# A two-layer decoder on one core: order of layers, score banks, units in flight and seven-product layers

## The chip, the cores and the metric

The kernel runs on one core of a Trainium2 chip. The metric is device time in microseconds (us) of that core. TensorE (PE) multiplies matrices and transposes; its results go to PSUM, of which the kernel uses eight banks of 128 x 512 fp32. VectorE (DVE) and ScalarE (ACT) read PSUM; GpSimd (POOL) doesn't in this kernel. SyncE (SP) issues most of the loads.

## What is computed

Six sublayers one after the other, each followed by a residual addition and a layer norm, all in fp32, on 16 sequences of 128 tokens with 256 features:

```python
x = _layernorm(x + attn0(x))       # 16 heads of 64, causal
x = _layernorm(x + xattn0(x))      # 8 experts, relu, gate made from ctx and itok: all 8 for every token
x = _layernorm(x + ffn0(x))        # 2 shared experts; 2 of 16 routed experts for each token
x = _layernorm(x + attn1(x))       # 16 heads of 16, keys within 8 of the query
x = _layernorm(x + xattn1(x, ctx)) # 16 heads of 16, keys and values from ctx
x = _layernorm(x + ffn1(x))        # 8 experts, gelu, gated sum: all 8 for every token
```

The experts of `xattn0` and `ffn1` each map 256 features to 512 and back.

## The kernel before

The 16 sequences are four groups (g = 0 to 3) of four sequences, 512 tokens. A piece of work is written (layer, g): (0,g) the first attention, (1,g) the first mixture of eight experts, (2,h) the routed mixture for half h, that is two groups at once, (3,g) and (4,g) the two attentions with 16-wide heads, (5,g) the last mixture of eight. A group passes its layers in order; (2,1) needs the routing of groups 2 and 3, so both (1,2) and (1,3), and (3,2) needs (2,1).

**Order.** Pieces are Python generators. They yield an estimated TensorE time, or a due time (`UNTIL`), or a condition. A planner (`Weaver.weave`) draws from a main stream (attention), a side stream called `dense` (mixtures) and a list of short ones (transposes, gates, routing plans, collecting results). Short streams go first; of main and side, the one with the smaller share of work done so far, each share divided by a given number of us. A stream that is not due, or whose condition doesn't hold, is passed over, and the other goes on and its share grows. The order so written is the priority of instructions; a scheduler of the language, in front of the chip, then fixes each engine's order and takes tiles' slots from pools, so an instruction that would lack a slot comes later. The dense order is a list near the end of the function (the line with `dense = Stream(chain(`), followed by the calls that weave: (0,0), (0,1) alone; (0,2), (0,3) with dense; then (3,0), (4,0); (3,1), (4,1); (3,2), (4,2), (3,3), (4,3); and what remains of dense.

**PSUM.** `bank` (L49) gives one bank for anything but attention scores, from six; scores take a pair of banks (tag S), of which there is one. So six and two make eight.

**16-wide attention.** `attention16` works through eight units of one sequence and half of the heads. For each, `scores` masks the keys by head on POOL (`kb`, L515), multiplies on TensorE and hands the scores to `softmax`, which on DVE and ACT makes a weight tile `e` (three slots, tag p); its scaling by `inv` (L380) is on POOL. Two steps later in the loop come the transposes of the weights (`weights_T`, ACT copy L390), one step after it the product with the values (`weigh`), and one more step later the output projection.

**Mixtures of eight.** `products` computes for each expert two matrix products. The second one (`multiply`, L836) always multiplies block matrices with seven products in place of eight, with block sums on DVE (L812 to L815); their weights' block sums are made on POOL once (L696 and L699) and kept in HBM. The first product, `hidden`, takes for each expert eight matmuls of 128x512 (each is two instructions in the trace), four banks, and one pass of DVE (L942, layer 1) or ACT (L1365, layer 5) per bank. With a `Firsts` object, the experts after the first use seven block products here too: 14 matmuls of 128x256, a bank `sums` that lives through the whole expert, two more banks, three ACT copies (L777, L782, L786), three DVE additions (L771), and the weights' sums (`weight_sums`, recorded at L720 and L746) as four POOL operations an expert; `rows_sums` adds four DVE operations per layer. Before, (5,2) and (5,3) have this, and no (1,g).

**Routed mixture.** `plan` ends with 16 scatters by indirect DMA on POOL (L1127); `experts0` runs two shared experts for two groups, then 16 pairs of routed tiles whose rows are loaded from what was scattered; `collect` gathers (L1303, POOL), adds and normalizes.

Of the kernel before, what the change touches and what calls it, by code (L numbers as in the profile page):

```python
# [8 lines left out]
F32 = mybir.dt.float32  # L9
# [5 lines left out]
P = 128  # L15
D = 256
# [6 lines left out]
T = GB * P  # L23
# [8 lines left out]
def kernel(ctx: ExitStack, tc: tile.TileContext, a: dict, out: bass.AP):  # L32
# [11 lines left out]
    ps = ctx.enter_context(tc.tile_pool(name="psum", bufs=2, space=bass.MemoryType.PSUM))  # L44
# [2 lines left out]


    def bank(tag):  # L49
        return ps.tile([P, T], F32, tag="B", name=f"ps{tag}", bufs=6)  # L50

    recent = [None]

# [8 lines left out]
    def joined(first):  # L62

        return nullcontext() if first else tc.high_priority()
# [38 lines left out]
    def load_quad(j):  # L103

        cols = slice(j * D, (j + 1) * D)
        return load_w(
            "attn", 2048, f"wquad{j}", a["L0_attn_W_Q"][:, :, cols], a["L0_attn_W_K"][:, :, cols],
            a["L0_attn_W_V"][:, :, cols], a["L0_attn_W_O"][:, 2 * j:2 * j + 2, :],
        )
# [206 lines left out]
    def project(pt, w, cols, xT):  # L316

        for c in range(KC):
            mm(pt, lhsT=w[:, c, cols], rhs=xT[:, c, :], start=c == 0, stop=c == KC - 1)
# [76 lines left out]
    def attention0(x, g):  # L396
        norm = Norm(x)
        norm.bias(bo0)

        def project_quad(g, j):  # L400
            wq, wk, wv, wo = first_quads[j] if g == 0 and j < 2 else load_quad(j)
            xT = xTs[g]
            qT = p2.tile([P, 2, T], F32, tag="qT", name="qT")
            kT = p2.tile([P, 2, T], F32, tag="kT", name="kT")
            for i in range(2):
                c = 2 * j + i
                cols = slice(i * P, (i + 1) * P)
                pq = bank("H")
                project(pq, wq, cols, xT)
                nc.vector.tensor_scalar(  # L410
                    qT[:, i, :], pq, bq0[:, c:c + 1], 0.125, ALU.add, ALU.mult
                )
                pk = bank("H")
                project(pk, wk, cols, xT)
                nc.scalar.activation(kT[:, i, :], pk, AF.Identity, bias=bk0[:, c:c + 1])
                yield 3.44

            v = yield from values(xT, wv, KC)
            heads0[g, j] = qT, kT, v, wo

        def scores(j, b):
            qT, kT, _, _ = heads0[g, j]
            at = slice(b * P, (b + 1) * P)
            s = ps.tile([P, 2, T], F32, tag="S", name="psS", bufs=1)[:, :, :D].rearrange(
                "p s (i k) -> p s i k", i=2
            )

            for i in range(2):
                for k in range(2):
                    rows = slice(64 * k, 64 * k + 64)  # L430
                    with joined(i == k == 0):
                        mm(
                            s[:, k, i, :], lhsT=qT[rows, i, at], rhs=kT[rows, i, at],
                            start=True, stop=True,
                        )
            return softmax(s, causal)

        def output(j, b, zT):
            po = bank("H")[:, :D]
            for i in range(2):  # L440
                mm(po, lhsT=zT[:, i, :], rhs=heads0[g, j][3][:, i, :], start=i == 0, stop=i == 1)
            norm.add(b, po, last=j == 3)

        if (g, 0) not in heads0:
            yield from project_quad(g, 0)
        units = [(j, b) for j in range(4) for b in range(GB)]
        e, eT, zT, at = {}, {}, {}, {}
        for n in range(len(units) + 5):
            if n < 16:
                j, b = units[n]  # L450
                e[n] = scores(j, b)
                at["e", n] = weaver.now + 9.0
                yield 0.6
            m = n - 2
            if m in e:
                yield UNTIL, at["e", m]
                eT[m], _ = weights_T(e.pop(m))
                at["t", m] = weaver.now + 2.5
                yield 0.5
            m = n - 5  # L460
            if m in zT:
                yield UNTIL, at["z", m]
                output(*units[m], zT.pop(m))
                yield 0.86
            m = n - 4
            if m in eT:
                j, b = units[m]
                yield UNTIL, at["t", m]

                pz = bank("O")[:, :D].rearrange("p (c q) -> p c q", c=2)  # L470
                got = eT.pop(m)
                for i in range(2):
                    for k in range(2):
                        h = 2 * i + k
                        with joined(h == 0):
                            mm(
                                pz[64 * k:64 * k + 64, i, :],
                                lhsT=heads0[g, j][2][:, b, 64 * h:64 * h + 64],
                                rhs=got[:, 2 * k + i, :], start=True, stop=True,
                            )  # L480
                zT[m] = p3.tile([P, 2, P], F32, tag="z", name="zT")

                nc.vector.tensor_tensor(  # L483
                    zT[m], pz, bv0[:, 2 * j:2 * j + 2].unsqueeze(2).to_broadcast([P, 2, P]), ALU.add
                )
                at["z", m] = weaver.now + 2.5
                yield 0.6
            if n < 16 and (n < 12 or g + 1 < NG):

                j, b = units[n]  # L490
                if b == 0:
                    ahead = project_quad(g, j + 1) if j < 3 else project_quad(g + 1, 0)
                yield next(ahead)
                if b == 3:
                    assert next(ahead, None) is None
        assert not e and not eT and not zT
        norm.done()


    def attention16(x, qT, kT, v, bv, wo, bo, seen):  # L500
# [9 lines left out]
        def scores(b, c):  # L510

            at = slice(b * P, (b + 1) * P)

            kb = p2.tile([P, 4, P], F32, tag="kb", name="kb")
            nc.gpsimd.tensor_tensor(  # L515
                kb, kT[:, c, at].unsqueeze(1).to_broadcast([P, 4, P]),
                hm4.unsqueeze(2).to_broadcast([P, 4, P]), ALU.mult,
            )
            yield UNTIL, weaver.now + 2.0
            s = ps.tile([P, 2, T], F32, tag="S", name="psS", bufs=1)  # L520
            s = s[:, :, :4 * keys].rearrange("p s (h k) -> p s h k", h=4)
            for k in range(2):
                rows = slice(64 * k, 64 * k + 64)
                for queries, key, _ in parts:
                    mine = slice(b * P + queries.start, b * P + queries.stop)
                    with joined(k == 0 and key == 0):
                        mm(
                            s[queries, k], lhsT=qT[rows, c, mine],
                            rhs=kb[rows, :, key:key + keys], start=True, stop=True,
                        )  # L530
            return softmax(s, seen)
# [37 lines left out]

        units = [(b, c) for b in range(GB) for c in range(2)]  # L570
        e, eT, zT, at = {}, {}, {}, {}
        for n in range(len(units) + 5):
            if n < 8:
                e[n] = yield from scores(*units[n])
                at["e", n] = weaver.now + 12.0
                yield 1.06
            m = n - 2
            if m in e:
                yield UNTIL, at["e", m]
                got = e.pop(m)  # L580
                eT[m] = [weights_T(got[:, 4 * k:4 * k + 4, :]) for k in range(2)]
                at["t", m] = weaver.now + 3.5
                yield 1.0
            m = n - 4
            if ("z", m) in at and units[m][1] == 1:
                yield UNTIL, at["z", m]
                output(units[m][0])
                yield 0.86
            m = n - 3
            if m in eT:  # L590
                yield UNTIL, at["t", m]
                weigh(*units[m], eT.pop(m))
                at["z", m] = weaver.now + 3.0
                yield 0.63
# [337 lines left out]
    def ensemble0(x, xT, g):  # L932
# [13 lines left out]
        def done(to, got, e, i, j):  # L946
# [10 lines left out]
            lambda t: after(  # L957
                products_end(t, norm, None, lambda norm, b: norm.done(b, 2)), tail(1, g)
            ),
            Firsts(xT, done) if g in () else None,  # L960
        )

    def small(tag, n=16, bufs=None):
# [391 lines left out]
    def experts1(x, xT, g, ng):  # L1355
# [16 lines left out]
        for b in range(GB):  # L1372
# [4 lines left out]
        yield from products(  # L1377
            load, lambda e: load_blocks(1, e, g, a["L1_ffn_w2"][e]), hidden,
            lambda t: after(products_end(t, norm, ng, lambda norm, b: store(norm, g, b))),
            Firsts(xT, done) if g in (2,3) else None,  # L1380
        )


# [69 lines left out]
    def begin(g):  # L1453
# [6 lines left out]

    weaver.short += [Stream(begin(g)) for g in range(NG)]
    dense = Stream(chain(
        (1, 0), (1, 1), (2, 0), (1, 2), (1, 3), (2, 1), (5, 0), (5, 1), (5, 2), (5, 3),
    ))
    weaver.short += [Stream(fill_tables()), Stream(sum_last_blocks())]
    weaver.weave(Stream(chain((0, 0), (0, 1))))
# [75 lines left out]
```

## Time and profile before

| | us |
|---|---|
| median of 3 runs | 1738.57 |
| lowest, highest | 1735.91, 1738.95 |
| the profiled execution | 1738.27 |
| its span, first to last instruction | 1736.6 |

The profile is of one execution. Where pieces lie in it, from the times of their own instructions:

| from | to | what runs |
|---|---|---|
| 0 | 217 | (0,0), (0,1) |
| 217 | 544 | (1,0), (1,1), with (0,2) and much of (0,3) |
| 544 | 610 | routing and scatters of half 0, rest of (0,3) |
| 610 | 676 | (2,0) |
| 676 | 1016 | (1,2), (1,3), with (3,0), (4,0), (3,1) |
| 1016 | 1146 | routing and scatters of half 1, (2,1), with (4,1) |
| 1146 | 1541 | (5,0), (5,1), start of (5,2), with (3,2), (4,2), (3,3), (4,3) |
| 1541 | 1736.6 | rest of (5,2), (5,3) |

Two more rows of the page, each digit the tenths of one fortieth of the span (43.4 us): how busy DVE is, and the clock that TensorE was granted.

```profile
DVE  4565565576677534878796875858769675965655
...
PEclk9999999999998899999999989999999999999998
```

In a groups row stand: line, engine, operation, output<-inputs, size of the weights, shape, count; after the bar the busy us of the group, the mean ns of one, the idle us of the engine just before them and what ended it. A matmul's ns include the end of its pipeline, so the next one starts before it is over. A stage row has start and end, length, then busy us (instructions) of PE, PE weight loads, DVE, ACT, POOL, then the granted clock, the DMA engines' share and GB/s. A chain row has start, length, and what the chain stood on.

### The profile page before, as it was taken

Reading aid. Unit: us, or ns where it says so; the run is one execution under the profiler, and the core shown is the slowest. Engines: PE = TensorE matmul, PEld = TensorE weight load, DVE = VectorE, ACT = ScalarE, POOL = GpSimd, SP = SyncE. Lnnn points to the kernel's source line nnn. Section 1 sums busy time; section 2 is a strip of 40 time slices with the busy share of each in tenths; the row PEclk is TensorE's granted clock in tenths of the full one; section 3 lists DMA queues with packets and bytes.
Section 4 is the critical chain, followed back from the end, with each engine's and each line's share of the span. In section 5 each row is a group of like instructions: output and inputs, shape, how many; then the busy total and the mean of one; then the engine's idle time right before and its main releaser. Section 6 shows DMA issues by size and latency. Waiting matters only on the chain.

```text
span 1736.6 us, 22830 instructions
## 1 busy us (share of the span) xinstructions
PE 1647.3 (95%) x8196; PEld 1080.5 (62%) x8196; DVE 1164.0 (67%) x2330; ACT 591.8 (34%) x1360; POOL 505.5 (29%) x543
## 2 busy tenths in 40 slices
PE   9999999999999799999899988998999999999996
PEld 6665656666656465656556655665665665588785
DVE  4565565576677534878796875858769675965655
ACT  4434411111022242103131212643846372654342
POOL 5443532220002302312241315334224132522220
PEclk9999999999998899999999989999999999999998
DMA  9533533432330458422223204671222221124330
GB/s 272 174 118 123 172 140 111 150 112 103 103 110 13 146 186 290 153 93 82 90 79 104 80 31 170 202 245 64 68 91 80 71 70 67 63 83 134 113 121 34
DMA packets 98192, 204.52 MB, mean 118 GB/s; under 512 B 16136, under 2 KB 58176, under 8 KB 98016
## 3 DMA queue, kind: packets, MB, share of 16 engines
q1 hardware_dynamic: 92176, 179.53, 31.2%
q0 software_dynamic: 5904, 23.54, 3.7%
q8 instruction: 65, 1.06, 0.2%
q14 instruction: 47, 0.39, 0.1%
HBM read 172.43 MB, written 37.81 MB: 121 GB/s over the span
## 4 chain that ended last, share of the span: by engine, by line
PE 75%; DVE 12%; DMA 4%; issue 3%; POOL 2%; ACT 1%; SPq 1%; another core or an unknown queue 0%; POOLq 0%; DVEq 0%; ACTq 0%
PE psH L55 40%; PE psM L55 21%; PE psO L60 5%; PE psS L55 4%; PE psO L55 3%; PE psH L60 2%; DVE nmax L358 1%; DVE e L364 1%; DMA wquad<-in_L_attn_W_Q 1%; DMA rows<-copies 1%; DVE total L370 1%; DVE x L311 1%; DVE x L293 1%; DVE acc L836 1%; POOL got L1303 1%
## 5 line engine op out<-in xcount | busy, mean ns | idle before, releaser
L55 PE MATMUL psH<-xT,we 128*128 128x512 f32 (+1 forms) x856 | 397.4, 590 | 0.5 <-DMA we<-in_L_xattn_proj_in 0.5
L380 POOL TENSOR_TENSOR e<-e,inv 128x512 f32<-128x512 f32 (+2 forms) x121 | 159.4, 1319 | 425.6 <-DVE inv L378 369.7
L55 PE MATMUL psM<-cm,wb 128*128 128x256 f32 x1024 | 263.6, 381 | 0.0
L55 PEld LDWEIGHTS psH<-xT,we 128*128 128x128 f32 x856 | 156.8, 191 | 137.0 <-issue 124.9
L55 PEld LDWEIGHTS psM<-cm,wb 128*128 128x128 f32 x1024 | 192.0, 190 | 52.2 <-issue 25.7
L55 PE MATMUL psM<-h,wb 128*128 128x256 f32 x768 | 200.8, 384 | 5.0 <-ACT h L1365 3.4
L836 DVE TENSOR_TENSOR acc<-psM,acc 128x512 f32<-128x512 f32 (+1 forms) x216 | 134.5, 624 | 98.3 <-PE psM L55 98.2
L390 ACT COPY eT<-psO 128x512 f32<-128x512 f32 (+1 forms) x192 | 105.5, 584 | 275.6 <-PE psO L60 261.3
L55 PEld LDWEIGHTS psM<-h,wb 128*128 128x128 f32 x768 | 143.0, 190 | 54.8 <-issue 29.3
L373 ACT ACTIVATE e<-e,nmax 128x128 f32<-128x128 f32 x256 | 99.5, 390 | 139.6 <-DVE nmax L358 113.4
L942 DVE SCALAR_TENSOR_TENSOR h<-psH,gt 128x512 f32<-128x512 f32 x128 | 87.6, 685 | 71.5 <-PE psH L55 71.2
L55 PE MATMUL psH<-xT,wquad 128*128 128x512 f32 x256 | 117.2, 601 | 6.1 <-DMA wquad<-in_L_attn_W_Q 5.4
L515 POOL TENSOR_TENSOR kb<-kT,hm 128x512 f32<-128x512 f32 x64 | 72.4, 1134 | 159.1 <-PE psS L55 104.5
L60 PEld LDWEIGHTS psO<-ident,e 128*128 128x128 f32 (+1 forms) x768 | 85.2, 133 | 48.2 <-issue 35.9
L60 PE MATMUL psO<-ident,e 128*128 128x128 f32 (+1 forms) x768 | 109.7, 280 | 2.0 <-POOL e L380 2.0
L1365 ACT ACTIVATE h<-psH,b 128x512 f32<-128x512 f32 (+1 forms) x100 | 60.6, 623 | 104.7 <-PE psH L55 95.9
L369 ACT ACTIVATE e<-e 128x576 f32<-128x576 f32 (+1 forms) x64 | 55.7, 871 | 88.2 <-DVE e L364 87.9
L55 PEld LDWEIGHTS psH<-xT,wquad 128*128 128x128 f32 x256 | 46.7, 190 | 58.9 <-issue 47.8
L309 POOL TENSOR_TENSOR rstd<-ve,mhalf 128x4 f32<-128x4 f32 (+1 forms) x32 | 28.9, 903 | 177.9 <-DVE ve L307 177.6
L370 DVE TENSOR_REDUCE total<-e 128x8 f32<-128x576 f32 (+1 forms) x64 | 62.8, 981 | 24.6 <-ACT e L369 24.0
L55 PE MATMUL psO<-eT,v 128*64 128x128 f32 (+2 forms) x1024 | 76.6, 313 | 0.0
L55 PE MATMUL psH<-wquad,zT 128*128 128x256 f32 x256 | 67.8, 388 | 4.8 <-DVE zT L483 2.5
(240 smaller groups left out, 2624.0 us busy)
## 6 DMA issues: line engine op xcount, KB each, us to landing
wb<-wbd SPq DMA_DIRECT2D x56, 896.0 KB
we<-in_L_xattn_proj_in SPq DMA_DIRECT2D x32, 512.0 KB
wt<-table SPq DMA_DIRECT2D x64, 256.0 KB
we<-in_L_ffn_w SPq DMA_DIRECT2D x32, 512.0 KB
wbd<-wb POOLq DMA_DIRECT2D x16, 896.0 KB
gt<-gatesd SPq DMA_DIRECT2D x32, 256.0 KB
results<-y SPq DMA_DIRECT2D x10, 768.0 KB
rows<-copies SPq DMA_DIRECT2D x6, 1024.0 KB
```

The costliest lines, as they stand in the source:

```text
L55: recent[0] = nc.tensor.matmul(*args, **how)
L60: return nc.tensor.transpose(out_, in_, ident[:n, :n])
L309: nc.gpsimd.tensor_tensor(rstd[:, at], ve[:, at], mhalf[:, at], ALU.pow)
L369: nc.scalar.activation(e, e, AF.Exp)
L370: nc.vector.tensor_reduce(total, e, AX.X, ALU.add)
L373: nc.scalar.activation(e[:, h, :], s[:, h // (n // 2), h % (n // 2), :], AF.Exp, bias=nmax[:, h:h + 1], accum_out=total[:, h:h + 1],)
L380: engine.tensor_tensor(e, e, inv.unsqueeze(2).to_broadcast([P, n, keys]), ALU.mult)
L390: return eT, nc.scalar.copy(eT, pt)
L515: nc.gpsimd.tensor_tensor(kb, kT[:, c, at].unsqueeze(1).to_broadcast([P, 4, P]), hm4.unsqueeze(2).to_broadcast([P, 4, P]), ALU.mult,)
L836: nc.vector.tensor_tensor(to, pm[:, :len(slots), :], to, ALU.add)
L942: nc.vector.scalar_tensor_tensor(out=h, in0=ph, scalar=0.0, in1=gates[e], op0=ALU.max, op1=ALU.mult)
L1365: nc.scalar.activation(to, one, AF.Gelu, bias=b1[:, 4 * e + c:4 * e + c + 1])
```

## The change

Five places change. The common banks go from six to four and the score pairs from one to two (in `attention0` as well as `attention16`). In `attention16` transposes, output and weighing of a unit come three, five and four steps after its scores, where they came two, four and three, and the loop has one step more. `Firsts` is given to (1,0), (1,1) and (5,1) too. In the dense order (5,0) stands before (2,1).

```diff
     def bank(tag):
-        return ps.tile([P, T], F32, tag="B", name=f"ps{tag}", bufs=6)
+        return ps.tile([P, T], F32, tag="B", name=f"ps{tag}", bufs=4)
...
-            s = ps.tile([P, 2, T], F32, tag="S", name="psS", bufs=1)[:, :, :D].rearrange(
+            s = ps.tile([P, 2, T], F32, tag="S", name="psS", bufs=2)[:, :, :D].rearrange(
...
-            s = ps.tile([P, 2, T], F32, tag="S", name="psS", bufs=1)
+            s = ps.tile([P, 2, T], F32, tag="S", name="psS", bufs=2)
...
-        for n in range(len(units) + 5):
+        for n in range(len(units) + 6):
...
-            m = n - 2
+            m = n - 3
             if m in e:
...
-            m = n - 4
+            m = n - 5
             if ("z", m) in at and units[m][1] == 1:
...
-            m = n - 3
+            m = n - 4
             if m in eT:
...
-            Firsts(xT, done) if g in () else None,
+            Firsts(xT, done) if g in (0,1) else None,
...
-            Firsts(xT, done) if g in (2,3) else None,
+            Firsts(xT, done) if g in (1,2,3) else None,
...
     dense = Stream(chain(
-        (1, 0), (1, 1), (2, 0), (1, 2), (1, 3), (2, 1), (5, 0), (5, 1), (5, 2), (5, 3),
+        (1, 0), (1, 1), (2, 0), (1, 2), (1, 3), (5, 0), (2, 1), (5, 1), (5, 2), (5, 3),
     ))
```

## The prediction

> **What bounds the kernel now.** I read the page's busy rows first, then a table of stages, then the chain of waits. The page's first row puts TensorE at the limit of the whole run:
>
> ```profile
> PE 1647.3 (95%) x8196; PEld 1080.5 (62%) x8196; DVE 1164.0 (67%) x2330; ACT 591.8 (34%) x1360; POOL 505.5 (29%) x543
> ```
>
> The stage table (start and end, length, busy time of each engine with its instructions, granted clock, DMA share, GB/s) shows where that fails:
>
> ```profile
> 217.00:544.00 327.00, 325.29 (x1393) 205.84 (x1391) 209.26 (x403) 53.97 (x191) 62.70 (x86) 1.00 0.32 112
> 544.00:610.00 66.00, 52.30 (x287) 34.97 (x287) 39.77 (x116) 22.55 (x86) 18.49 (x19) 0.84 0.29 96
> 610.00:676.00 66.00, 60.46 (x342) 42.74 (x341) 24.20 (x66) 27.11 (x76) 0.00 (x0) 0.95 0.67 229
> 1016.00:1146.00 130.00, 110.37 (x620) 72.32 (x619) 84.94 (x202) 51.21 (x118) 44.05 (x36) 0.89 0.49 160
> 1200.00:1541.00 341.00, 331.34 (x1723) 204.91 (x1722) 257.05 (x460) 192.75 (x263) 111.88 (x92) 0.99 0.22 75
> ```
>
> To price a stage I need matmul work, not busy time. A gapless stretch near the end of the chain gives the unit:
>
> ```profile
> 1690.12 2.59 PE psM L55 x12
> ...
> 1696.16 3.45 PE psM L55 x16
> ```
>
> All of these are 128x256, so one takes 0.216 us. The timeline's start-to-start of the 128x512 ones is 0.43 us, of full 128x128 ones 0.109; the tiled small ones I count at 0.03 to 0.23, also from start-to-start. Counting each stage's forms at these prices gives work and loss: 217 to 544, 309 and 18; 544 to 610, 40 and 26; 610 to 676, 49 and 17; 676 to 1016, 313 and 27; 1016 to 1146, 88 and 42; 1146 to 1541, 357 and 38; the rest, 176 and 20. With 38 before 217, some 1512 is work and 225 is loss.
>
> The largest loss, 1016 to 1146, is in the chain of waits of that stage:
>
> ```profile
> 1034.16 10.69 PE psH L55 x20
> ...
> 1046.58 20.94 issue
> ...
> 1072.39 6.96 DMA wt<-table
> ```
>
> Mixture (1,3) has ended, (2,1) needs its plan and its sixteen scatters, and only the attention (4,1) is left. Its key masks and softmax scaling are on POOL, which sits behind those scatters (16 x 0.96 us). Here the Trainium skill (Perfetto Trace Analysis, Identifying the Most-Contended Engine) calls matmul busy time a bad measure and asks for LDWEIGHTS busy. By the busy row this stage loses 19.6 us. LDWEIGHTS is busy 56% of it, and 88% in the gapless end (80.5 of 92 us), which would make the loss 47. My count, 42, keeps the forms apart, and I use it.
>
> **Sevens in three more layers, (1,0), (1,1), (5,1).** Each of seven experts of a layer trades 16 instructions of 128x512 (6.88 us) for 28 of 128x256 (6.04 us): 0.84 x 7 x 3 = 17.6 us less work. What they add is read from (5,2) and (5,3):
>
> ```profile
> L771 DVE TENSOR_TENSOR h<-psM,h x42: 640/692/692, 1523.8 to 1711.7; 128x512 f32<-128x512 f32 x42
> ...
> L720 POOL TENSOR_TENSOR sw<-we x28: 723/728/982, 1470.9 to 1686.6; 128x256 f32<-128x256 f32 x28
> ```
>
> DVE: 3 x 0.69 per expert and 4 x 0.42 per layer, 16 us a layer. POOL: 4 x 0.73 = 2.9 per expert. ACT: 3 x 0.58 per expert. In 217 to 544 DVE goes from 209 to 241 in about 315 us, 77%; POOL and ACT have room. TensorE covers them while attention (0,2), (0,3) has work to offer; with that cover gone each late addition would cost its 0.69 us, 29 us for two layers at the very worst. In (5,1) the weight sums on POOL queue between the sixteen gathers of (2,1) (0.96 each, behind the landing of the results, 4.9 us): at most one expert late. I take 2.6 us of stalls in all, so -15; bounds -18 and 0.
>
> **(5,0) ahead of (2,1).** (5,0) depends on (4,0), normalized at 929, so it can start at 1016. Its loads (0.5 MB and 0.9 MB an expert, 11 MB in all) pass on SP ahead of (2,1)'s row and table loads; at a DMA share of 0.49 they fit, and (2,1)'s loads no longer wait for the scatters. On POOL it issues three additions at the end (0.8 us each), so the scatters don't hold it. Beside it runs (4,1): 103 + 29 = 132 us of work, loss taken as 8. Then (2,1) stands alone, for (3,2) needs its result. The trace has that case: (2,0) alone, 610 to 676, lost 17. From its end to the first projections of (3,2) took some 45 us before (gathers, norm, transposes); (5,1) covers it. After that (3,2) to (4,3) have only what is left of (5,1), some 50 us, and (5,2), 97, beside 124 of their own, where they had some 210 before. The planner's shares count what dense work ran while they were blocked, so attention now goes first and dense pieces fill its due times, about 30 us a layer; some of (5,2) should be left to cover the start of (5,3). Loss for the stage: 38 before, 45 after, for the mix is tighter. Sum: 42 + 38 against 8 + 17 + 45, so -10; bounds -34 (nothing more lost in the lone stage or the tighter mix) and +20.
>
> **Two score banks, four common ones.** Waits of score matmuls for a reader of the one bank, from the groups view (5.5 and 3.9 and 2.2 us):
>
> ```profile
> L55 PE MATMUL psS<-kT,qT 64*128 64x128 f32 x512 | 47.0, 303 | 5.5 <-DVE e L352 5.5
> L55 PE MATMUL psS<-kb,qT 64*128 64x512 f32 x128 | 37.2, 657 | 7.5 <-DVE e L364 3.9 <-issue 3.4
> L55 PE MATMUL psS<-kb,qT 64*64 64x288 f32 x256 | 22.9, 427 | 2.4 <-DVE e L352 2.2 <-DVE inv L378 0.2
> ```
>
> 11.6 us is the most this can return; part turns into the next wait, so -4. Against it stands the skill's same page (Optimization Strategy): repeated gaps on the engine that should be full can mean too little SBUF or PSUM for the next tile, and this edit takes two of six common banks. Pairing each group of matmuls with its reader in the timeline, a bank of the main forms lives 1.7 to 3.5 us; four or more are in use 1% of 217 to 544, 15% of 1155 to 1268, 7 to 10% up to 1448 and 0 to 6% of most other stages, 65 us in all. By the rule all of that is exposed, and if a third of it stalls it costs 22; by the pairing a fifth bank is seldom asked for. A layer of sevens in the gapless end had at most two of these plus its own two. I take +6, bounds 0 and +22.
>
> **Three 16-wide units in flight.** No instruction is added; transposes, weighing and output of a unit come one step later in the order. Nothing in the trace shows a fourth softmax tile, and there are still three of tag p, so the fourth unit's softmax waits on the first one's transposes; behind that wait on DVE would stand other evacuations, each under 1.2 us. TensorE's waits for softmax results in these layers are small (2.0 for `e` on L380, 3.0 for `zT`). I take -2, bounds -8 and +6.
>
> **Sum.** -15 - 10 - 4 + 6 - 2 = -25. The profiled execution took 1738.27 (span 1736.6, 1.7 around it) and the median is 1738.57, so the two agree to 0.3: 1713.
>
> **The rivals.** About 0.2%, 3.5 us, is what a measurement of this kernel can tell from no change.
> - *The holes close fully* (0.17). (2,1)'s gaps find work, the tighter mix loses nothing: order -34, the rest -15, near 1689. For: PE loses only 18 in 217 to 544, where two streams of work run. Against: (2,0) alone did lose 17.
> - *The sevens are eaten by DVE and the late order gains nothing* (0.18). DVE is at 75% in 1200 to 1541 and 83% from 850 to 1016; if the additions come late TensorE gets 6 of 17.6, order -2, score banks -4, common banks +6, units -2: near 1730. Against: the gapless end shows the sevens themselves costing no gap.
> - *No change* (0.07). Only the reordering's loss cancels it all, 1735 to 1742: the order doesn't do what it says because (3,2) starts about 70 us later.
> - *Slower, by the attention chain* (0.13). From (2,1)'s end to (4,3)'s norm it took 395 us (1146 to 1541). (2,1) would now end near 1212 (1016, less 10 for the sevens before it, plus 140 and 66); with 121 us behind the chain ((5,3) with its end 109, its transposes and gate 12, uncovered) the kernel breaks even at 404. Were the chain set by latency, not by TensorE, and each of its four layers lengthened 6 us by missing banks, it takes 419, a span of 1752 and a time of 1754. For: nothing but (5,1) and (5,2) can cover it. Against: PE is busy 331 of 341 there with 310 of work, and over 60 us of that dense work has gone elsewhere, so it should shrink toward 345.
>
> **How the numbers follow.** The case of the sum, 1700 to 1725, has 0.45. Faster is 0.45 + 0.17 + 0.18 = 0.80, same 0.07, slower 0.13. The range 1692 to 1738 takes in the first three cases and half of no change, leaving out the chain rival and the best end.
>
> **What would show it.** The 42 us hole at the end of (1,3) gone, with first-product work of (5,0) at once behind it; a lone (2,1) of about 66 us, some 1146 to 1212; 336 instructions of 128x512 fewer and 588 of 128x256 more, over three layers; psS waits for DVE under 5 us; no new waits of `psH` or `psM` matmuls for their readers over 10 us. I am wrong if TensorE idles after the last (4,3) unit, if L771 leaves ACT and TensorE waiting in (1,0) and (1,1), or if bank waits pass 20 us.

## The result and the profile after

The changed kernel takes 1751.20 us, median of 5 runs (1749.95 to 1755.85), against 1738.95 of the kernel before in the same measurement: a ratio of 1.0077, with a 95% interval of 1.0061 to 1.0094. By the ratio it is slower by 13 us, where 25 us less were forecast. The profiled execution, the slowest of the five, took 1755.85 us, its span 1754.2, so the two profiled spans differ by 17.6 us.

TensorE has less to do, and its busy row hardly changes (1647.3 before):

```profile
PE 1645.9 (94%) x8448; PEld 1129.2 (64%) x8448; DVE 1221.8 (70%) x2412; ACT 637.2 (36%) x1455; POOL 564.4 (32%) x620
```

252 matmul instructions more (588 of 128x256 in, 336 of 128x512 out) are less work: counted at the prices of the prediction, 1494 us where it was 1512. So the loss, time in which TensorE doesn't work at full clock, went from 225 to 260. Here it is by stage, work and loss in us:

| stage | before | work, loss | after | work, loss | loss forecast |
|---|---|---|---|---|---|
| to the end of (0,1) | 0 to 217 | 179, 38 | 0 to 212 | 178, 34 | 34 |
| to the end of (1,1) | 217 to 544 | 309, 18 | 212 to 528 | 296, 20 | 20 |
| plan of half 0, (2,0) | 544 to 676 | 89, 43 | 528 to 663 | 91, 44 | 43 |
| (1,2), (1,3) | 676 to 1016 | 313, 27 | 663 to 1012 | 316, 33 | 25 |
| then | 1016 to 1146, (2,1) with (4,1) | 88, 42 | 1012 to 1174, (5,0) with (4,1) | 143, 19 | 8 |
| | | | 1174 to 1243, (2,1) alone | 52, 17 | 17 |
| to (4,3)'s norm | 1146 to 1541 | 357, 38 | 1243 to 1613 | 301, 69 | 45 |
| the rest | 1541 to 1737 | 176, 20 | 1613 to 1755 | 118, 24 | 20 |

(The column on the right divides the forecast's terms over the stages; 6 us for banks were not placed.) In the stage rows of the kernel after, columns as before, the lone (2,1) behaves like the lone (2,0), and the stage of the last attention layers has lost clock as well:

```profile
1012.00:1174.00 162.00, 151.49 (x659) 94.55 (x659) 115.20 (x238) 68.68 (x92) 36.96 (x35) 0.97 0.30 100
1174.00:1243.00 69.00, 61.91 (x346) 42.63 (x345) 29.67 (x88) 28.01 (x77) 1.40 (x2) 0.98 0.69 231
1238.00:1613.00 375.00, 342.03 (x1881) 238.01 (x1882) 286.11 (x510) 209.45 (x344) 166.97 (x152) 0.96 0.23 77
1613.00:1754.00 141.00, 121.24 (x555) 101.25 (x553) 89.37 (x177) 47.03 (x96) 31.97 (x39) 0.96 0.26 89
```

The same two stages before, from (2,1)'s last pair to (4,3)'s norm and on to the end:

```profile
1140.00:1541.00 401.00, 386.87 (x1938) 237.98 (x1938) 294.68 (x555) 209.95 (x291) 138.04 (x115) 0.99 0.26 88
1541.00:1737.00 196.00, 178.34 (x821) 152.08 (x819) 117.53 (x227) 72.87 (x150) 42.22 (x55) 0.96 0.29 96
```

(2,1) ends 98 us later, the attention layers behind it take only 26 us less, and what follows them 55 less: 17 us in all. The signs by which the forecast was to be known came with this loss all the same: the hole behind (1,3) is mostly gone (loss 42 to 19), (2,1) runs alone for 69 us, and the instruction counts are as said. They show that the edits took effect, not that they pay. Score matmuls wait less for DVE, 4.7 us where it was 11.6:

```profile
L55 PE MATMUL psS<-kT,qT 64*128 64x128 f32 x512 | 46.2, 302 | 2.4 <-DVE e L352 2.0 <-issue 0.3
L55 PE MATMUL psS<-kb,qT 64*128 64x512 f32 x128 | 36.1, 641 | 3.2 <-issue 2.4 <-DVE e L364 0.7
L55 PE MATMUL psS<-kb,qT 64*64 64x288 f32 x256 | 22.7, 427 | 2.0 <-DVE e L352 2.0
```

But a kind of wait appears that the kernel before hardly had: a matmul that waits for the reader of somebody else's tile. TensorE's waits, from 663 to 1012 and, behind the dots, from 1243 to 1454 (total, times, longest):

```profile
PE psO L55 <- DVE acc L836: 1.2, 1, 1.2
PE psH L60 <- DVE h L942: 0.9, 1, 0.9
PE psO L55 <- DVE h L942: 0.8, 1, 0.8
...
PE psM L55 <- DVE h L771: 2.8, 2, 2.1
PE psH L55 <- POOL sw L720: 2.8, 1, 2.8
PE psO L55 <- ACT h L1365: 2.6, 1, 2.6
PE psH L55 <- ACT h L1365: 2.2, 1, 2.2
```

A product with values, `psO`, takes nothing from an expert's hidden tile `h`. It waits for the bank that the operation writing `h` has read and gives back. With six common banks (the first kernel below) no `psO` waits for an `h` any more. `psM <- h L771` and `psH <- sw L720` are different: there the sevens of (5,1) wait for their own additions and weight sums.

### The profile page after: what moved, and what is told of

The parts are those of the page before. It is cut to its first block, busy times and chain, and to the rows that moved or that the text cites. A ratio compares the mean times of both kernels' runs of the same rounds, so it can differ in the third digit from the quotient of the medians.

```text
span 1754.2 us, 23714 instructions
## 1 busy us (share of the span) xinstructions
PE 1645.9 (94%) x8448; PEld 1129.2 (64%) x8448; DVE 1221.8 (70%) x2412; ACT 637.2 (36%) x1455; POOL 564.4 (32%) x620
## 4 chain that ended last, share of the span: by engine, by line
PE 66%; DVE 20%; DMA 3%; ACT 3%; issue 3%; POOL 2%; another core or an unknown queue 1%; SPq 1%; POOLq 0%; DVEq 0%; ACTq 0%
PE psH L55 34%; PE psM L55 22%; PE psO L60 3%; PE psO L55 3%; DVE e L364 2%; DVE nmax L358 2%; PE psS L55 2%; DVE total L370 2%; PE psH L60 2%; DVE acc L836 1%; DVE cm L812 1%; DVE cm L814 1%; DVE cm L813 1%; DVE x L311 1%; DMA rows<-copies 1%
## 5 line engine op out<-in xcount | busy, mean ns | idle before, releaser
L55 PE MATMUL psM<-cm,wb 128*128 128x256 f32 x1024 | 266.9, 385 | 4.3 <-DVE cm L812 2.4
L55 PE MATMUL psH<-xT,we 128*128 128x512 f32 (+1 forms) x604 | 259.0, 557 | 7.0 <-ACT h L1365 2.2
L380 POOL TENSOR_TENSOR e<-e,inv 128x512 f32<-128x512 f32 (+2 forms) x114 | 150.4, 1320 | 301.8 <-DVE inv L378 266.9
L55 PEld LDWEIGHTS psM<-cm,wb 128*128 128x128 f32 x1024 | 191.9, 191 | 52.1 <-issue 14.1
L55 PE MATMUL psM<-h,wb 128*128 128x256 f32 x768 | 206.0, 392 | 4.5 <-ACT eT L390 2.0
L55 PEld LDWEIGHTS psH<-xT,we 128*128 128x128 f32 x604 | 112.7, 193 | 97.8 <-issue 77.9
L55 PEld LDWEIGHTS psM<-h,wb 128*128 128x128 f32 x768 | 145.6, 194 | 46.3 <-issue 16.4
L55 PE MATMUL psH<-xT,wquad 128*128 128x512 f32 x256 | 119.0, 609 | 3.9 <-DMA wquad<-in_L_attn_W_Q 3.5
L60 PE MATMUL psO<-ident,e 128*128 128x128 f32 (+1 forms) x768 | 112.1, 280 | 8.8 <-ACT eT L390 4.4
L60 PEld LDWEIGHTS psO<-ident,e 128*128 128x128 f32 (+1 forms) x768 | 85.2, 133 | 52.2 <-issue 24.9
L771 DVE TENSOR_TENSOR h<-psM,h 128x512 f32<-128x512 f32 x105 | 72.1, 687 | 42.4 <-PE psM L55 40.2
L720 POOL TENSOR_TENSOR sw<-we 128x256 f32<-128x256 f32 x70 | 56.5, 807 | 115.9 <-PE psM L55 92.3
L55 PE MATMUL psO<-eT,v 128*64 128x128 f32 (+2 forms) x1024 | 77.1, 315 | 9.4 <-ACT h L1365 4.7
L1303 POOL DMA_INDIRECT got<-results,r_places x32 | 31.9, 996 | 166.5 <-DMA we<-in_L_xattn_proj_in 84.6
L55 PEld LDWEIGHTS psH<-xT,wquad 128*128 128x128 f32 x256 | 47.3, 192 | 56.9 <-issue 50.6
L1365 ACT ACTIVATE h<-h,b 128x256 f32<-128x256 f32 x126 | 57.5, 501 | 70.2 <-DVE h L771 64.7
```

The costliest lines, as they stand in the source:

```text
L55: recent[0] = nc.tensor.matmul(*args, **how)
L60: return nc.tensor.transpose(out_, in_, ident[:n, :n])
L380: engine.tensor_tensor(e, e, inv.unsqueeze(2).to_broadcast([P, n, keys]), ALU.mult)
L720: engine.tensor_tensor(to, one, two, ALU.subtract)
L771: nc.vector.tensor_tensor(block(i, j), other, block(i, j), ALU.add)
L1365: nc.scalar.activation(to, one, AF.Gelu, bias=b1[:, 4 * e + c:4 * e + c + 1])
```

## The experiments

Each ratio is to the kernel before, run on the same chip in the same measurement, with its 95% interval. "Undone" edits start from the changed kernel, "alone" ones from the kernel before. All leave the computation as it is. The kernel before took 1730 us in the measurement of the first four kernels and 1739 to 1740 in the others, so ratios are compared here, not times. The traces place this difference ahead of (2,0), and not by edit but by measurement: from the start of the last scatter of half 0, those four reach the first matmul of the shared experts within 2 us, and all the others, the kernel before and the changed one among them, after 9 to 14. In the changed kernel's trace ScalarE stands still for 16.1 us there; for what, the trace doesn't name.

Theory A was: four common banks are too few. Theory B: the later (2,1) makes the last four attention layers a chain bound by latency. Theory C: sevens in (5,1) load DVE and ACT beside attention.

### One part undone

Banks as before (the score tile of `attention0` likewise):

```diff
-        return ps.tile([P, T], F32, tag="B", name=f"ps{tag}", bufs=4)
+        return ps.tile([P, T], F32, tag="B", name=f"ps{tag}", bufs=6)
...
-            s = ps.tile([P, 2, T], F32, tag="S", name="psS", bufs=2)
+            s = ps.tile([P, 2, T], F32, tag="S", name="psS", bufs=1)
```

> The changed kernel with its banks as before: six common ones and one pair for scores. Theory A (four common banks are too few once sevens hold one through a whole expert beside attention; matmuls wait for readers of unrelated tiles): the waits on readers of other tiles after 1243 go, time 1712 to 1728. Theory B (the later (2,1) makes the four last attention layers a chain bound by latency): the banks matter little, 1743 to 1755. Theory C (sevens in (5,1) load DVE and ACT beside attention): 1740 to 1752.

Measured 1.0042 (1.0019 to 1.0064). Of the 0.77% some 0.35 goes, where A wanted more than the whole. On the 1739 us of the first measurement it would be 1746, which B and C both allow.

The old order:

```diff
-        (1, 0), (1, 1), (2, 0), (1, 2), (1, 3), (5, 0), (2, 1), (5, 1), (5, 2), (5, 3),
+        (1, 0), (1, 1), (2, 0), (1, 2), (1, 3), (2, 1), (5, 0), (5, 1), (5, 2), (5, 3),
```

> The changed kernel with the old order, (2,1) ahead of (5,0). Theory A: the hole of 42 us at 1016 comes back, the bank waits stay, so 1748 to 1765. Theory B: the chain is started 70 us earlier and covered by (5,0), (5,1) and part of (5,2), so 1715 to 1730. Theory C: 1745 to 1758, as (5,1) still runs beside attention.

Measured 1.0031 (1.0019 to 1.0043). A wanted it slower; the order costs. But B alone wanted 1% or more to go.

Two units in flight again (steps n - 2, n - 4, n - 3, and one loop step less):

```diff
-            m = n - 3
+            m = n - 2
             if m in e:
...
```

> The changed kernel with two 16-wide units in flight. Theories A, B and C all put it within 6 us of 1751. If three units in flight were what costs (transposes, weighing and output come later in the order and hold their banks and tiles longer), it is 1735 or less.

Measured 1.0181 (1.0156 to 1.0205). None of the theories as written had this: the depth, which I had booked at -2 us, saves 1.0% in this company. In the traces the chain from (2,1)'s last matmul to (4,3)'s norm takes 392 us with two units and 373 with three.

Eight products in (5,1):

```diff
-            Firsts(xT, done) if g in (1,2,3) else None,
+            Firsts(xT, done) if g in (2,3) else None,
```

> The changed kernel with eight products in (5,1), sevens in (1,0), (1,1), (5,2), (5,3). Theory C: 1730 to 1740, since (3,2) and (4,2) then share DVE and ACT with lighter work. Theory A: part of it, 1743 to 1752 (a bank less is held, but 6 us of work come back). Theory B: (5,1) is longer cover, 1745 to 1752.

Measured 1.0016 (1.0000 to 1.0033): 6 us of matmul work come back and the kernel gets 0.6% faster. On 1739 us that is 1742, between what C and what A and B wanted, so the time alone doesn't decide. The stage does: the rows from (2,1)'s end to (4,2)'s norm, first with eight products in (5,1), then the changed kernel's:

```profile
1233.00:1430.00 197.00, 185.00 (x895) 111.11 (x894) 144.79 (x266) 91.28 (x126) 83.58 (x68) 0.97 0.27 94
```

```profile
1243.00:1454.00 211.00, 188.04 (x982) 130.02 (x981) 159.32 (x286) 105.28 (x174) 103.08 (x96) 0.94 0.27 88
```

The sevens put 14.5 us more on DVE, 14.0 on ACT and 19.5 on POOL, and the stage is 14 us longer. That speaks for C.

### One part alone

Banks (both score tiles):

```diff
-        return ps.tile([P, T], F32, tag="B", name=f"ps{tag}", bufs=6)
+        return ps.tile([P, T], F32, tag="B", name=f"ps{tag}", bufs=4)
...
-            s = ps.tile([P, 2, T], F32, tag="S", name="psS", bufs=1)
+            s = ps.tile([P, 2, T], F32, tag="S", name="psS", bufs=2)
```

> The kernel before with four common banks and two pairs for scores, nothing else. If four banks are too few by themselves it is 1.005 to 1.012 of before. If they cost only where sevens run beside attention (which undoing shows in the sum: 0.35% less), it is 0.998 to 1.003. If a second pair for scores frees attention, 0.990 to 0.997.

Measured 1.0072 (1.0051 to 1.0092): the swap costs by itself.

Four common banks, one score pair:

```diff
-        return ps.tile([P, T], F32, tag="B", name=f"ps{tag}", bufs=6)
+        return ps.tile([P, T], F32, tag="B", name=f"ps{tag}", bufs=4)
```

> The kernel before with four common banks and still one pair for scores: two banks of PSUM unused. If the 0.72% of the swap of banks is the missing common banks, this is 1.007 to 1.015, the second pair giving some back; if the second pair itself disturbs the order, 0.999 to 1.004.

Measured 1.0140 (1.0121 to 1.0159). So the two missing banks cost 1.4%, 24 us, and the second pair gives back 0.7%, 12 us. TensorE's waits of this kernel from 1010 to 1460 again name readers of banks, most of them of other tiles:

```profile
PE psM L55 <- DVE acc L836: 2.6, 1, 2.6
...
PE psO L60 <- DVE x L291: 1.7, 1, 1.7
PE psH L60 <- DVE zT L559: 1.4, 1, 1.4
...
PE psO L60 <- DVE acc L836: 0.6, 1, 0.6
```

They sum to a few us only. The rest is not in waits that the trace names. The scheduler that fixes each engine's order knows of the four slots and puts off what would lack one, which fits what is seen, though it was not tried apart: work simply comes later, (4,1)'s norm at 1160 where it was 1155, (3,2)'s at 1280 (1269), (4,3)'s at 1562 (1541).

Order:

```diff
-        (1, 0), (1, 1), (2, 0), (1, 2), (1, 3), (2, 1), (5, 0), (5, 1), (5, 2), (5, 3),
+        (1, 0), (1, 1), (2, 0), (1, 2), (1, 3), (5, 0), (2, 1), (5, 1), (5, 2), (5, 3),
```

> The kernel before with (5,0) ahead of (2,1), nothing else. Theory B (the four last attention layers are a chain that starts later and has less work beside it): 1.004 to 1.015 of before. The prediction's sum (the hole at 1016 filled, the later stage hardly worse): 0.992 to 0.996.

Measured 1.0108 (1.0057 to 1.0159), against the prediction's term of -10 us and for B. From (2,1)'s last pair to (4,3)'s norm, and to the end:

```profile
1243.00:1624.00 381.00, 349.07 (x1856) 227.87 (x1856) 285.71 (x501) 204.35 (x311) 147.77 (x128) 0.98 0.24 80
1624.00:1753.00 129.00, 109.17 (x496) 90.82 (x495) 77.39 (x165) 42.41 (x85) 28.25 (x35) 0.94 0.26 86
```

By the same count of forms this stage has 323 us of work, 39 less than before, and is 20 us shorter: its loss went from 39 to 58. The longest of TensorE's waits in it are for weight tiles of attention, `PE psO L60 <- POOL e L380`, 13.5 us in five waits.

Depth (and one loop step more):

```diff
-            m = n - 2
+            m = n - 3
             if m in e:
...
-            m = n - 4
+            m = n - 5
...
-            m = n - 3
+            m = n - 4
```

> The kernel before with three 16-wide units in flight, nothing else. If depth alone is what gains (undoing it in the changed kernel cost 1%): 0.988 to 0.994. If it gains only with the second pair of score banks, since one pair is handed from unit to unit, or only where the cover is thin: 0.997 to 1.004.

Measured 1.0044 (1.0031 to 1.0056): alone it costs.

Depth and banks, the two edits shown above, together.

> The kernel before with four common banks, two score pairs and three 16-wide units in flight. Alone these gave 1.0072 and 1.0044. If they are independent, 1.010 to 1.013. If depth pays once there are two score pairs (undoing the depth in the changed kernel cost 1.0%): 0.992 to 1.000.

Measured 1.0082 (1.0062 to 1.0102). A second score pair doesn't make depth pay, so that is not where the 1.0% comes from.

Depth and order, likewise.

> The kernel before with the new order and three 16-wide units in flight; banks and sevens as before. If the new order costs because the last four attention layers are a chain bound by latency, depth shortens it: 1.002 to 1.008 of before, where the order alone gave 1.0108. If the two costs are independent (1.0108 and 1.0044): 1.013 to 1.018.

Measured 1.0046 (1.0028 to 1.0065), where the two alone would sum to 1.015. Depth costs 0.4% in the old order and saves 0.6% in the new one, with banks and sevens as before. The two intervals in the new order overlap a little (1.0057 to 1.0065), but the pair with all else changed, 1.0181 and 1.0077, agrees and is clear. That speaks for B: depth lets an attention layer run further ahead of its own softmax, and only in the new order does that shorten the kernel. In the old order, too, the chain behind (2,1) takes 387 us instead of 397 with it, but (2,1) ends 10 us later and what follows the chain is 8 us longer. The stage in the new order, 361 us for the same layers instead of 381:

```profile
1247.00:1608.00 361.00, 337.49 (x1796) 216.46 (x1796) 270.32 (x486) 196.67 (x299) 145.15 (x124) 0.98 0.24 80
```

Sevens in (1,0) and (1,1):

```diff
-            Firsts(xT, done) if g in () else None,
+            Firsts(xT, done) if g in (0,1) else None,
```

> The kernel before with sevens in (1,0) and (1,1), nothing else. The prediction's term, 12 us of matmul work less and under 3 of stalls: 0.993 to 0.996 of before. If the chain of attention sets the end of this stage too, or DVE's additions come late: 0.998 to 1.004.

Measured 0.9966 (0.9950 to 0.9981), 6 us: half of the work that it takes away. In its own stages nearly all of it arrives (rows of this kernel; the two took 329 us before, 318 here):

```profile
218.00:378.00 160.00, 159.80 (x755) 118.53 (x754) 118.61 (x211) 36.90 (x107) 74.38 (x105) 1.00 0.39 134
378.00:536.00 158.00, 157.87 (x812) 120.11 (x812) 122.28 (x245) 39.94 (x124) 34.19 (x36) 1.00 0.30 94
```

It is given back later: (1,3) is done 11 us earlier, but (4,0)'s norm comes at 928 where it was 929, and (4,3)'s at 1548 where it was 1541. Only what follows is shorter, 184 us instead of 196.

Sevens in (5,1):

```diff
-            Firsts(xT, done) if g in (2,3) else None,
+            Firsts(xT, done) if g in (1,2,3) else None,
```

> The kernel before with sevens in (5,1) too, nothing else; in the old order (5,1) runs beside (4,2) and (3,3). The prediction's term (6 us of matmul work less, little of it stalled): 0.996 to 0.999 of before. If the added DVE and ACT work beside 16-wide attention costs more than the matmul work saves (the changed kernel got 0.6% faster without it): 1.001 to 1.006.

Measured 0.9998 (0.9984 to 1.0011): nothing, the least that I had allowed this layer.

### Sevens, banks and combinations

Banks as before and eight products in (5,1): the first and the last of the four edits that undo, together.

> The changed kernel with six common banks and one score pair, and eight products in (5,1). With sevens in (5,1) and these banks it was 1.0042. If those sevens cost through the bank they hold, six banks hide it and this is 1.003 to 1.008; if through VectorE and ScalarE beside attention, 0.996 to 1.001.

Measured 0.9988 (0.9972 to 1.0004). With six banks the sevens of (5,1) cost 0.54% (1.0042 less 0.9988), as much as with four (0.61%). The stage from (2,1)'s end to (4,2)'s norm shows it again, with six banks and sevens in (5,1), then without:

```profile
1232.00:1440.00 208.00, 185.29 (x981) 129.73 (x980) 162.61 (x287) 105.10 (x173) 103.20 (x97) 0.94 0.27 88
```

```profile
1243.00:1432.00 189.00, 179.96 (x896) 108.38 (x895) 142.62 (x266) 90.60 (x125) 82.92 (x68) 0.99 0.28 97
```

So it is not for want of banks that they cost; what is left is their work on DVE, ACT and POOL, 20, 14.5 and 20 us here, or the order that the edit brings. These were not tried apart.

Eight products in (5,1) and in (5,2):

```diff
-            Firsts(xT, done) if g in (1,2,3) else None,
+            Firsts(xT, done) if g in (3,) else None,
```

> The changed kernel with sevens in (1,0), (1,1), (5,3) and eight products in (5,1) and (5,2), the two that run beside the last attention layers. 12 us more matmul work than the changed kernel. If sevens beside attention cost more than they save: 1.000 to 1.003 of before or less, no more than the kernel with eight in (5,1) alone (1.0016). If the stage is bound by matmul work: 1.004 to 1.008.

Measured 1.0039 (1.0016 to 1.0061), between the two. Taking the sevens from (5,2) as well doesn't go on helping. They lie beside (3,3) and (4,3) and, for some 30 us, alone.

The old order and eight products in (5,1), the rest as changed: again two of those edits together.

> The changed kernel in the old order and with eight products in (5,1): banks, depth and the sevens in (1,0) and (1,1) stay. If the order and the sevens of (5,1) are what costs, each about 0.5%, this is 0.994 to 0.999 of before; if the banks remain a cost of their own in this company, 1.000 to 1.006.

Measured 1.0070 (1.0051 to 1.0090): the banks remain a cost of their own. The single parts in it sum to 0.82%.

All sevens on the kernel before, nothing else:

```diff
-            Firsts(xT, done) if g in () else None,
+            Firsts(xT, done) if g in (0,1) else None,
...
-            Firsts(xT, done) if g in (2,3) else None,
+            Firsts(xT, done) if g in (1,2,3) else None,
```

> The kernel before with sevens in all three more layers and nothing else of the change. Alone, (1,0) and (1,1) gave 0.9966 and (5,1) 0.9998. If they add up: 0.995 to 0.998. If the 18 us less of matmul work let the attention chain set the end: 0.998 to 1.002.

Measured 0.9955 (0.9939 to 0.9971), 1729.99 us against 1739.40: faster than both kernels by 8 us and more. Its interval overlaps that of (1,0) and (1,1) alone, so the third layer's share is not shown.

## Why the prediction was wrong, by its own steps

**What bounds the kernel.** Right as a reading of before, wrong as a guide: 17.7 us less work bought 8 us on the kernel before and nothing here, for the loss, 225 us of the old span, grew by 35 and decided.

**Sevens, -15.** Work right, and in (1,0), (1,1) the stalls too (loss from 18 to 20). The term was mis-sized in what became of it: 6 of 12 us reach the end alone, and in (5,1) nothing in the old order. In the new order the sevens of (5,1) cost some 10 us. "At most one expert late" held for POOL's sums, with one wait of 2.8 us. What fails is "2.6 us of stalls in all": 14 us each of ACT and DVE beside the softmax of (3,2) and (4,2) were counted, and their delay of attention was put at nothing.

**Order, -10.** The failed step, and the largest miss of any term: alone it is +1.08%, 19 us. Of its terms the lone (2,1) was exact, 17. "(5,0) beside (4,1), loss taken as 8" measured 20 in the kernel with the order alone and 19 in the changed one, where the stage took 162 us, not 140: the plan's short matmuls stand ahead of (5,0) in TensorE's order and wait for DVE's routing, `PE psH L55 <- DVE r_one L1011`, 6.3 us there and 5.3 in the changed kernel, and 10.2 us at half clock follow in both. The hole was not only a lack of other work. "45 after, for the mix is tighter" measured 62 with the order alone (56 to (4,3)'s norm and 6 up to the end of (5,2)) and 69 in the changed kernel up to that norm. The chain has less beside it and doesn't shrink with it: 401 us before, 381 and 375 after, not the 345 of the rival's counter-argument. Some of (5,2) was left when the chain ended, as forecast (32 us of it), so it wasn't cover that ran out; TensorE stood idle with dense work still to do, because what was next in its order waited. So the term that failed is the loss behind (2,1), taken as 45 and measured as 62 to 69.

**Score banks -4, common banks +6.** Both sizes too small by a factor: -12 and +24. I weighed the rule of the Trainium skill (Perfetto Trace Analysis, Optimization Strategy) that repeated gaps can mean too little PSUM for the next tile against my pairing of banks with readers, and took the pairing. The estimate under the rule, the upper bound, was 22; the measurement is 24. The pairing counted how many banks were in use in an order that had been fixed with six. With four the order itself is another.

**Depth, -2.** Alone +8 us, just outside my bound of +6; in the new order -11 (1.0108 to 1.0046). Its worth hangs on whether the attention chain is on the path.

**Rivals.** The one on the slower side named the mechanism for which the runs speak, a chain bound by latency, and the time: 1754, measured 1751, the profiled execution 1756. That the time came out is luck: (2,1) ended at 1243, not 1212, the chain took 370 us from there, not 419, and 141 us, not 121, lay behind it, and these three misses cancel. Missing banks do lengthen the chain (397 to 414 us with four common banks alone), but in the changed kernel it got shorter all the same. I gave it 0.13 because TensorE was busy 331 of 341 us in that stage before. That is the busy row which the same text had called a bad measure; by count its work was 310. The kernel before already lost 31 us there, beside enough dense work, and that was the sign.

**The parts together.** Alone they sum to 1.88%. Depth and order together give 1.06% less than their sum, which brings it to 0.82, near the measured 0.77. Not settled: some combinations miss such a sum by 0.3 to 0.7% (old order with all else changed, 1.0031 where 0.80% was due; eight products in (5,1), 1.0016 where 0.84% was due). Sevens in (5,1) even seem to help where the banks and the depth are changed in the old order (1.0070 without, 1.0031 with). Every edit gives a new fixed order on each engine, and how much of such differences is one order's luck was not tried.

## What to carry to other kernels

Before moving a piece of independent work into a hole, find the longest dependent chain that the move starts later, and measure that chain with less work beside it; a stage that loses time while other work is at hand may be bound by the chain, whatever its busy row says. Where a scheduler fixes the order from the number of slots, slots in use in the old trace are no bound for the cost of fewer. Work taken off the busiest engine and put on the engines that feed the chain can cost more than it saves, and the same edit can pay in one place and cost in another.

## What the hardware showed

TensorE's clock made the short waits dearer. In the stage 1238 to 1613 the granted clock is 0.96, where it was 0.99 before. By the trace's record of the clock it was half for 27.3 us there and for 10.2 us before. That costs at most half of this time, 14 and 5 us: up to 9 of the 31 us by which the loss of this stage grew. No wait of a matmul listed from 1243 to 1613 is longer than 2.8 us, and in two places gaps of 2.4 and 2.9 us from one matmul's start to the next were enough: after the one of 2.4 us at 1319 the clock is half for 6.8 us, after the one of 2.9 at 1347 again. It is no rule: after a gap of 2.8 us at 1057 the clock stayed full. Three rows of the kernel after show it, the middle one without such a gap:

```profile
1317.00:1330.00 13.00, 9.45 (x54) 6.53 (x56) 8.17 (x14) 10.78 (x18) 4.18 (x4) 0.74 0.15 63
1330.00:1345.00 15.00, 15.00 (x123) 11.46 (x120) 12.17 (x23) 11.08 (x21) 5.03 (x6) 1.00 0.11 35
1345.00:1358.00 13.00, 10.42 (x68) 7.93 (x67) 6.73 (x14) 7.54 (x13) 1.60 (x2) 0.74 0.20 72
```
